# First AUGRU gates through the attention's two PSUM banks, and the keys of step 3 loaded in the phase change

## The chip, the cores and the metric

The kernel runs on one core of a Trainium2 chip. The metric is the device time of one execution in microseconds. Before the change it was 2062.48 us (median of 5 runs, 2060.84 to 2063.89).

## What is computed

A recommender block over 1024 users with a history of 100 steps of 128 features: a GRU over the history, an attention over the GRU's outputs ("keys"), a second GRU whose update gate is scaled by the attention (AUGRU), and a small MLP. Cut to what matters here:

```python
_, gru_seq = jax.lax.scan(gru_step, h0, swapaxes(history, 0, 1))
keys = swapaxes(gru_seq, 0, 1)
...
attn = softmax(where(mask == 1, score, -inf), axis=1)[..., 0]
pooled = einsum('bt,btd->bd', attn, keys)
att_seq = pooled.T[:T]                 # one weight per step and user
def augru_step(h, inp):
    x_t, a_t = inp
    ti = concatenate([h, x_t], axis=-1)
    r = sigmoid(ti @ aug_Wr.T + aug_br)
    u = sigmoid(ti @ aug_Wu.T + aug_bu)
    h_hat = tanh(concatenate([h * r, x_t], axis=-1) @ aug_Wh.T + aug_bh)
    u = a_t[:, None] * u
    h_new = (1.0 - u) * h + u * h_hat
```

The weight `a_t` of step t is feature t of the pooled vector, so no AUGRU state can be formed before the pooling over all 100 steps is complete. With h = 0 the first step needs only the gates of `x_0` and `a_0`: h = a_0 * sigmoid(u) * tanh(h_hat).

## The kernel before

Everything is fp32, features on the 128 partitions and users along the free dimension, in two halves of 512 users (`i` = 0, 1). There are two phases, each written out by hand: the order of the calls in the program is the order of the instructions in each engine's queue, and an instruction waits by semaphore for what it reads and for the last reader of the buffer or PSUM bank that it writes.

**The GRU phase** (`gru_phase`) runs 100 steps of the GRU, and beside them the attention's MLP, the softmax in blocks and the pooling. It holds six PSUM banks for gates (0 to 5) and two for the attention (6 and 7). After the last step the six banks are handed out again for the end of the attention: bank 2 and its neighbours hold products of the pooling (`kw`, L599 and L600), scores and exponents. The attention's two banks are read last by ACT at L704. DVE pools half 1, POOL half 0. At the end L937 (DVE) writes the pooled rows of half 1 and then half 0 into `s_b`, and eight stores, four for each half, bring them to `pooled_d` in DRAM: L941 issues half 1's four and one of half 0's on SP's queue; the other three of half 0 are issued on ACT's queue at L1204, in the next phase.

**The AUGRU phase** (`augru_phase`) sorts users by length, so that later steps run over fewer columns. Its widths come from a table, one of three (two lines, one line, full width), chosen by a branch at L1251 and L1252. The inputs take the two-line table. The phase starts so:

1. `load_key(0, i)`: four PE transposes (L1036) of gathered GRU outputs into one PSUM bank, and a copy by ACT (L1037) into a `k3` tile.
2. `first_step(i)`: for each half two matmuls (L977, `pu` and `ph`) and ACT's sigmoid and tanh on them (L979). Each of the four has a bank of its own, `EARLY_BANKS` = 2, 5, 6, 0.
3. `load_key(1, i)`, then the three stores on ACT's queue (L1204), then `gather_weights`: eight gathers on POOL (L144, `att_r`), four for each half, which read `pooled_d` in sorted order.
4. `open_gates(1, 1)` and `open_gates(1, 0)`: the key's part of step 1's three gates for each half, six matmuls (L1050), then `load_key(2, i)`.
5. `first_state(0)`: the row of weights of step 0 is spread over the partitions by four matmuls with the identity (L992) from half 0's `att_r`, and DVE makes the state of half 0 (L1003, L1004). `first_weights(0)` does the same for step 1's weights. Half 1 follows inside the first half step.
6. The loop over steps 1 to 99, with a `half_step` for each half: the state's part of the gates (L1054), ACT's sigmoids (L1074, L1075) and tanh (L1062), DVE's products (L1078 to L1091), the opening of the next gates, and the loads of step t + 2 (`load_att`, `load_key`). From step 8 on the keys come as rows that POOL gathers (L168, paced by a copy of the last `rest`, L167) and that DVE transposes (L1040).

The PSUM banks of this phase are seven pools of one bank (`ps3_0` to `ps3_6`) and `pa3` with one. By their places in PSUM `ps3_6` and `pa3` are the attention's two banks, and `ps3_0` to `ps3_5` the six others. `bank(name, n)` takes bank n; without n the next of a ring.

## Time and profile before

| | us |
|---|---|
| median of 5 runs | 2062.48 (2060.84 to 2063.89) |
| the profiled execution | 2061.72 |
| its span (first to last instruction) | 2059.8 |
| PE busy in it | 2026.3 |
| DVE / POOL / ACT busy | 1749.4 / 1303.3 / 831.0 |
| mean granted clock of PE | 0.995 |
| last transposes of the GRU phase's end to the first gates: PE without work | 1437.1 to 1447.1 |

The profile is of one execution. A row names an engine, a line, the tile written and those read, and a duration; the figure in brackets is the idle time of the engine before it and who ended it. "issue" means that the profile shows nobody for it. PE is TensorE, PEld its weight loads, ACT ScalarE, POOL GpSimd, and SPq or ACTq a DMA issued on that queue. The fp32 matmul stands in it as two rows (x2). PE's granted clock is 1 at full speed and 0.5 at half.

### The profile page before, as it was taken

The numbers are of one execution on the slowest core, as the hardware profiler recorded it, in microseconds if no ns is written. First come the engines' busy times: TensorE is split into PE (matmuls) and PEld (weight loads), VectorE is DVE, ScalarE is ACT, GpSimd is POOL, SyncE is SP. The second block draws the span as 40 slices with busy tenths as digits, with TensorE's granted clock in tenths as the row PEclk, the third lists the DMA queues.
The fourth block names the chain that finished last, engine by engine and source line by source line (L and its number), as shares of the span: only waits on it lengthen the run. The fifth ranks groups of instructions, "written<-read, shape, count | busy, mean of one in ns | idle before, by whom it ended". The sixth has DMA issues, their size and how long they took to land. (4 is left out here: it accounts for less than half of the span.)

```text
span 2059.8 us, 26800 instructions
## 1 busy us (share of the span) xinstructions
PE 2026.3 (98%) x8320; PEld 978.7 (48%) x8320; DVE 1749.4 (85%) x3050; ACT 831.0 (40%) x1516; POOL 1303.3 (63%) x1299
## 2 busy tenths in 40 slices
PE   8999999999999999999999999998899999999997
PEld 3343333333333333333333333334444556679997
DVE  6888999998989888988889888999467777888886
ACT  3333343333433343433333343343344444455554
POOL 0233939669796959596897868898545444444332
PEclk9999999999999999999999999999899999999999
DMA  4643333323334333333333333323334333333332
GB/s 119 117 94 89 103 103 97 93 81 97 111 106 103 116 107 114 111 106 102 103 98 95 104 96 96 104 90 114 107 102 113 96 92 96 94 97 101 88 77 36
DMA packets 254132, 204.36 MB, mean 99 GB/s; under 512 B 76006, under 2 KB 217034, under 8 KB 253978
## 3 DMA queue, kind: packets, MB, share of 16 engines
q1 hardware_dynamic: 240266, 170.43, 29.4%
q0 software_dynamic: 12128, 31.91, 5.5%
q8 instruction: 68, 1.11, 0.2%
q14 instruction: 86, 0.70, 0.1%
q10 hardware_dynamic: 1584, 0.20, 0.1%
HBM read 146.43 MB, written 54.40 MB: 97 GB/s over the span
## 5 line engine op out<-in xcount | busy, mean ns | idle before, releaser
L501 PE MATMUL ps<-x,wih 128*128 128x512 f32 x1200 | 592.8, 603 | 4.0 <-DMA x<-in_hist_x 4.0
L501 PE MATMUL ps<-hn,whh 128*128 128x512 f32 x1188 | 574.4, 592 | 0.0
L501 PEld LDWEIGHTS ps<-x,wih 128*128 128x128 f32 x1200 | 220.9, 191 | 327.7 <-issue 252.3
L501 PEld LDWEIGHTS ps<-hn,whh 128*128 128x128 f32 x1188 | 225.7, 190 | 284.2 <-issue 274.3
L487 POOL TENSOR_TENSOR xm<-x,m 128x512 f32<-128x512 f32 x200 | 248.7, 1244 | 137.2 <-DMA m<-mask_d 136.9
L532 ACT ACTIVATE ps<-ps,bih 128x512 f32<-128x512 f32 x200 | 132.4, 662 | 479.4 <-DVE ps L531 479.4
L513 ACT ACTIVATE r<-ps,brz 128x512 f32<-128x512 f32 x200 | 137.5, 688 | 380.0 <-PE ps L501 379.2
L488 POOL TENSOR_TENSOR hist<-hist,xm 128x512 f32<-128x512 f32 x200 | 267.8, 1339 | 15.7
L600 POOL TENSOR_TENSOR pooled<-pooled,kw 128x512 f32<-128x512 f32 x191 | 254.3, 1332 | 15.0
L599 POOL TENSOR_TENSOR kw<-kt,e 128x512 f32<-128x512 f32 x191 | 219.1, 1147 | 64.7 <-DVE e L772 64.6
L168 POOL DMA_INDIRECT rows<-keys_d,idx_k x204 | 198.7, 974 | 82.1 <-POOL rows L167 50.4
L576 DVE TENSOR_TENSOR kq<-hn,item 128x512 f32<-128x512 f32 x200 | 226.3, 1171 | 0.0
L663 PE MATMUL pm<-hn,wk 128*32 128x512 f32 x1200 | 211.8, 596 | 3.2 <-ACT q L242 1.6
L663 PE MATMUL pm<-kq,wkq 128*32 128x512 f32 x1200 | 209.4, 592 | 0.0
L1062 ACT ACTIVATE c<-ph,bh 128x96 f32<-128x96 f32 (+41 forms) x198 | 96.5, 487 | 254.5 <-PE ph L1054 229.4
L663 PE MATMUL pm<-mv,w 128*32 128x512 f32 (+1 forms) x808 | 196.3, 598 | 0.9 <-DVE e L753 0.9
L697 DVE TENSOR_TENSOR f<-pm,q 128x512 f32<-128x512 f32 x200 | 128.3, 683 | 52.7 <-PE pm L663 52.5
L167 POOL COPY rows<-rest 128x1 f32<-128x1 f32 x204 | 38.6, 189 | 202.1 <-DVE rest L1091 197.9
L1078 DVE TENSOR_TENSOR pu<-pu,c 128x96 f32<-128x96 f32 (+41 forms) x197 | 88.3, 448 | 91.3 <-ACT c L1062 82.2
L536 DVE TENSOR_TENSOR d<-hn,ps 128x512 f32<-128x512 f32 x198 | 135.9, 687 | 34.9 <-ACT ps L532 32.5
L537 DVE TENSOR_TENSOR d<-ps,d 128x512 f32<-128x512 f32 x200 | 138.3, 692 | 23.7 <-ACT ps L533 6.8
L531 DVE TENSOR_TENSOR ps<-ps,u 128x512 f32<-128x512 f32 x200 | 140.0, 700 | 21.6 <-PE ps L501 0.5
(180 smaller groups left out, 3017.7 us busy)
## 6 DMA issues: line engine op xcount, KB each, us to landing
x<-in_hist_x SPq DMA_DIRECT2D x212, 256.0 KB
keys_d<-kt SPq DMA_DIRECT2D x46, 1024.0 KB
m<-mask_d SPq DMA_DIRECT2D x200, 128.0 KB
keys_d<-kt SPq DMA_DIRECT2D x64, 64.0 KB
rows<-keys_d,idx_k POOLq DMA_INDIRECT x204
s_b<-mv SPq DMA_DIRECT2D x200, 8.0 KB
at<-att_d SPq DMA_DIRECT2D x34, 48.0 KB
mask_i<-in_mask SPq DMA_DIRECT2D x8, 200.0 KB
```

The costliest lines, as they stand in the source:

```text
L168: nc.gpsimd.indirect_dma_start(out=r[:, k, :], out_offset=None, in_=keys_d[q], in_offset=bass.IndirectOffsetOnAxis(ap=idx_k[:, k, i : i + ...
L487: nc.gpsimd.tensor_mul(d, x, m)
L488: nc.gpsimd.tensor_add(acc, acc, d)
L501: nc.tensor.matmul(p, lhsT=w[:, g, :], rhs=v, start=(j == 0), stop=(j == len(parts) - 1),)
L513: nc.scalar.activation(r, pr, AF.Sigmoid, bias=brz[:, 0:1])
L531: nc.vector.tensor_add(pi, pi, u)
L536: nc.vector.tensor_sub(d, h, pi)
L537: nc.vector.tensor_mul(d, pz, d)
L576: nc.vector.tensor_mul(kq, h, item[:, self.cols])
L599: eng.tensor_mul(d, k, w)
L600: eng.tensor_add(acc, acc, d)
L663: nc.tensor.matmul(p[i][s, :], lhsT=w[:, s], rhs=v, start=start, stop=stop)
```

## The change

```diff
-EARLY_BANKS, LATE_BANKS = (2, 5, 6, 0), (3, 4, 1)
+FREE_BANK, EARLY_BANKS, LATE_BANKS = 6, (2, 5, 6, 0), (3, 4, 1)
...
-        qp = pools.enter_context(tc.tile_pool(name="qp3", bufs=3 * NH))
+        qp = pools.enter_context(tc.tile_pool(name="qp3", bufs=4 * NH))
...
             for j, (n, f) in enumerate((("u", AF.Sigmoid), ("h", AF.Tanh))):
-                p = bank(f"p{n}", EARLY_BANKS[NH * i + j])
+                if j:
+                    p = pa.tile([P, HB], F32, tag="a", name=f"p{n}")
+                else:
+                    p = bank(f"p{n}", FREE_BANK)
...
-            if t + 2 < T:
+            if 1 < t < T - 2:
                 load_key(t + 2, i)
...
         for i in range(NH):
-            load_key(0, i, (None, EARLY_BANKS[NH])[i])
+            load_key(0, i, (None, FREE_BANK)[i])
         gates = [first_step(i) for i in range(NH)]
         for i in range(NH):
-            load_key(1, i, (EARLY_BANKS[0], None)[i])
+            load_key(1, i, (FREE_BANK, None)[i])
         for to, t in later["att", 0][: G - 1]:
             nc.scalar.dma_start(out=to, in_=t)
         sorted_rows = [gather_weights(i) for i in range(NH)]
+        for i in range(NH):
+            load_key(2, i, (FREE_BANK, None)[i])
         open_gates(1, 1, EARLY_BANKS)
         open_gates(1, 0, LATE_BANKS)
         for i in range(NH):
-            load_key(2, i)
+            load_key(3, i)
```

The first gates and the transposes of the keys of steps 0, 1 and 2 all go through banks 6 and 7. The keys of step 2 are transposed ahead of step 1's gates and not behind them. The keys of step 3 are loaded in the phase change, through bank 7, and no longer in the two half steps of step 1. There are two more `k3` tiles. In the changed kernel the lines of the AUGRU phase stand four to six lower: L977 is L981, L1036 L1040, L1037 L1041, L992 L996, L1054 L1058, L1204 L1208.

## Prediction

> **What bounds the kernel now.** I read the page first, then a table of six stretches around the phase change, then the timeline there. The page:

> ```profile
> span 2059.8 us, 26800 instructions
> PE 2026.3 (98%) x8320; PEld 978.7 (48%) x8320; DVE 1749.4 (85%) x3050; ACT 831.0 (40%) x1516; POOL 1303.3 (63%) x1299
> PEclk9999999999999999999999999999899999999999
> ```

> PE is the bound: 98% busy, and in the slices its one dip before the end, with the one lower clock digit, is where the GRU phase hands over to the AUGRU phase, about 1440 us. So only what shortens PE's stream, or the stretch in which PE has no work, can count. The stretches (us; length, then busy PE, PEld, DVE, ACT, POOL; granted clock, DMA share, GB/s):

> ```profile
> 1437.10:1447.10 10.00, 0.00 (x0) 0.00 (x0) 9.11 (x23) 2.84 (x5) 9.38 (x9) 0.65 0.56 169
> 1447.10:1457.30 10.20, 9.29 (x24) 4.50 (x25) 1.27 (x2) 3.71 (x6) 0.00 (x0) 0.84 0.30 51
> 1457.30:1463.70 6.40, 4.26 (x21) 2.38 (x19) 0.00 (x0) 1.16 (x2) 4.85 (x6) 1.00 0.15 41
> 1463.70:1471.40 7.70, 7.61 (x32) 5.09 (x32) 4.10 (x7) 2.54 (x5) 2.80 (x3) 0.78 0.21 53
> 1480.00:1500.00 20.00, 20.00 (x61) 9.79 (x60) 12.29 (x20) 8.74 (x15) 16.12 (x29) 1.00 0.60 187
> ```

> PE does nothing for 10 us. In the next 10 us it works, while DVE and POOL stand almost still, so its work there isn't obviously on the path. After 1480 it is full. Which chain crosses? The timeline (start, length, engine, line; idle before in brackets):

> ```profile
> 1446.36 0.69 DVE L600 TENSOR_TENSOR pooled<-pooled,last 128x512 f32<-128x512 f32 x1
> 1447.08 1.29 DVE L937 TENSOR_TENSOR s_b<-used,pooled 128x512 f32<-128x512 uint8 x2
> 1447.15 2.05 PE L977 MATMUL pu<-k,wu 128*128 128x512 f32 x2 [10.07 <-issue]
> 1447.80 2.49 SPq L941 DMA_DIRECT2D pooled_d<-s_b  x5
> 1452.46 0.69 ACT L979 ACTIVATE first_h<-ph,bh 128x512 f32<-128x512 f32 x1 [0.17 <-PE ph L977]
> 1453.39 0.35 ACTq L1204 DMA_DIRECT2D pooled_d<-s_b  x1
> 1453.79 1.05 ACTq L1204 DMA_DIRECT2D pooled_d<-s_b  x2
> 1457.33 0.99 POOL L144 DMA_INDIRECT att_r<-pooled_d,idx  x1 [10.46 <-issue]
> 1463.70 0.51 PE L992 MATMUL first<-ident,att_r 128*128 128x128 f32 x2 [0.75 <-DMA att_r<-pooled_d,idx]
> 1465.05 0.69 DVE L1004 TENSOR_TENSOR h<-first,first_h 128x512 f32<-128x512 f32 x1
> 1471.42 1.12 PE L1054 MATMUL pr<-h,wr 128*128 128x510 f32 x2
> ```

> The profile says "issue" for PE's 10.07 us. In the order of the program the first gate matmul waits for the count that the last DVE L600 sets; that ends at 1446.36 + 0.69 = 1447.05, and PE starts 0.10 later: bank 2, which the gate writes, was a pooling buffer until then. ACT therefore finishes the four first gates at 1453.15 and dispatches the key copies of step 1 by 1453.4. Behind these in ACT's queue stand three of the eight stores of the pooled rows, though their data was ready when the second L937 ended, at 1448.37. POOL's gathers need all eight stores. So the path is: DVE pooling, gates, ACT's queue, stores, gathers, first state, and from 1471.42 PE back to back.

> **The change, part by part.** *First gates in banks 6 and 7.* These were the attention's, whose last reader (ACT L704) ends at 1429.86; the wait for DVE leaves the first gate, which now waits for ACT's second key copy (end 1440.02). One 512-column gate is two passes: 0.43 us each at full clock, 0.85 at half clock (rows of 1450.54 and 1447.15). ACT has loaded its table by 1441.32. With two banks for four gates, PE waits for ACT's 0.69 us twice. At the clocks that I expect (half from 1440.6 to 1444.0, after 3.5 us without work as in the row of before), the gates' matmuls end about 1445.3, ACT's last gate 1446.2, the key copies of step 1 are dispatched by 1447.0. [...] I take the row: the stores issue at 1448.4 to 1449.85 (their 1.45 us of before), and **what is late next is DVE's pooling**.

> *The stores.* SP's five end issuing at 1450.29 as before; ACT's three now go out beside them. In a table of stretches of a quarter us, the DMA share falls to nothing at 1451.27 after SP's five and at 1455.8 after ACT's three: 0.98 and 0.96 us from issue end to last byte. If issue alone counted, the last byte would come at 1451.3: 4.5 us earlier. [...] That is 1455.8 - 1451.8 = **4.0 us** earlier. I take 4.0, with 3.0 and 4.6 as ends. POOL has waits for all eight in a row, and from last byte to its first gather it took 1.5 us; I leave that.

> *Gathers, first state.* Eight gathers at 1.26 us on POOL, landing about 1.5 us after each: nothing changes, all move by 4.0. First landing of half 0 complete: 1459.7 instead of 1463.70. No other DMA is moved past: SP's order is the same, and POOL's L168 row gathers start after the same `rest`.

> *PE until then.* After the gates: keys of steps 1, 2, then six gates of step 1 (5.1 us), then keys of step 3. The keys of step 2 are copied by ACT behind its stores, at 1449.9 to 1451.1; the third gate of half 1 shares bank 6 and waits for the first of these copies, about 0.7 us; behind it stand three gates and step 3's keys. Key 3 goes twice through one bank: (0.44 + 0.2 + 0.58) x 2 = 2.4 us. PE and ACT are done about 1456.6. The cover is the gathers' flight to 1459.7, 3.1 us of slack: cost nothing. If PE ran at half clock throughout, six gates take 10.2 us from 1448.2, and with the keys it ends about 1461.5: 1.8 us of the gain lost.

> *Keys of step 3 out of step 1.* Two times 0.44 us of PE (four transposes) and 0.58 of ACT leave. The first (1469.80) goes where PE then waits anyway for half 1's state (DVE, 1471.36): nothing. The second (1477.11) lies in the back-to-back stretch: **0.44 us**, full. The two more `k3` buffers bring no instruction, and no new late wait stands in the program: nothing.

> *Clock at the first half step.* By the granted clock in stretches of 1 us PE was at half clock from about 1464.0 to 1467.4, after sparse work. It will be sparse again for the same 4 us of gathers, so I expect the same. Ends: 0.3 us less, since half 1's gathers land only by 1468.6, or one window more, 3.4 x 0.5 = 1.7 us more. I take 0.

> Sum: 4.0 + 0.44 = 4.4, rounded with POOL's shorter row of waits after ACT's last store to 4.5 us. The profiled execution took 2061.72 (span 2059.8, 1.9 around it), so 2057.2 for it; the median of the runs is 0.8 higher, 2062.48, so **2058.0**. From 1480 on PE is full, so the shift is carried to the end.

> **The rivals.**
> A, as summed: 2058.0, chance 0.68. For it: the 0.10 us between DVE's end and PE's start, and the row of ACT's stores right behind ACT's gates. Its own spread (stores 3.0 to 4.6, clock) is 2056.5 to 2059.4.

> B, the gap isn't the bank's: PE stood for another reason (its code still to come, while DMA was full to 1442.7, for one), and the stores leave ACT as late as before. Then only the keys count: 2062.0, chance 0.09. Against it: ACT went through its branch, copied keys and loaded its table in that time.

> C, PE becomes the late one: at half clock through the six gates, it loses 1.8 of 4.5, or the first half step pays one more window, 1.7: about 2059.7, chance 0.18. For it: the work before the gathers is more broken up than before. Against it: six gates in a row from 1448 to 1454, enough by the row (3.3 us) to raise the clock.

> D, slower: the clock stays at half into the steps, because PE's work is thinner from 1440 to 1460. Each us of half clock in the full stretch costs 0.5; it takes 9 us to undo the gain, 17 us for 2066.7. The longest half-clock stretch with work in this trace is 3.5 us. Chance 0.05, about 2067.

> **How the numbers follow.** A measurement of this kernel can tell about 0.2%, 4.1 us, from no change; faster means below 2058.4. A lies just beyond that: I give about 0.49 of its 0.68 to faster, and C's lower edge 0.01: 0.50. Same: the rest of A and C, and B: 0.45. Slower: 0.05. The range of 8 in 10 takes A whole and C: 2056.2 to 2060.4; B and D are left out.

> **What would show it.** Right: PE's first gate at about 1440.2 with no wait for DVE; L1208's three stores at 1448.4 to 1449.9, beside SP's; DMA share near 1 from 1448.7 to 1451.8; POOL's first `att_r` gather at 1453.3 (1457.33); the last of half 0's `first` transposes at about 1459.7; no `pk` in step 1; every step from 2 on 4.4 us earlier. Wrong: a first gate still at 1447; `first` transposes waiting for ACT's key copies instead of the gathers (C); half clock beyond 4 us of work after the first state (C, D); stores that end after 1452.5.

## The result, and the profile after

The changed kernel takes 2058.15 us (median of 26 runs, 2056.66 to 2060.78), beside 2061.88 for the kernel before (46 runs). The ratio is 0.9982, with an interval of 0.9976 to 0.9987: 3.7 us faster, between 2.7 and 4.9. The gain is clear of the noise, but a little short of the 0.2% (4.1 us) from which on the prediction calls a kernel faster; by that bound it falls under "same", to which the prediction gave 0.45, and 0.50 to "faster". The predicted time was 2058.0.

The page of the changed kernel:

```profile
span 2056.5 us, 26797 instructions
PE 2027.3 (99%) x8320; PEld 978.7 (48%) x8320; DVE 1750.8 (85%) x3050; ACT 829.7 (40%) x1516; POOL 1300.6 (63%) x1299
PEclk9999999999999999999999999999999999999999
```

The span is 3.3 us shorter, and the one slice with a lower clock digit is gone (in the second execution of the changed kernel, below, it is there again). PE has the same 8320 matmuls and is busy 1.0 us longer (2027.3 against 2026.3), so the time has come out of PE's waiting: 29.2 us of the span instead of 33.5. The timeline of the changed kernel around the phase change shows where (start, length, engine, line, operation; in brackets the idle time before and its releaser):

```profile
1440.70 1.40 PE L981 MATMUL pu<-k,wu 128*128 128x512 f32 x2 [3.04 <-ACT k L1041]
1446.13 0.69 ACT L983 ACTIVATE first_h<-ph,bh 128x512 f32<-128x512 f32 x1 [0.17 <-PE ph L981]
1447.66 1.29 DVE L937 TENSOR_TENSOR s_b<-used,pooled 128x512 f32<-128x512 uint8 x2
1448.38 2.54 SPq L941 DMA_DIRECT2D pooled_d<-s_b  x5
1448.99 1.49 ACTq L1208 DMA_DIRECT2D pooled_d<-s_b  x3
1453.98 0.99 POOL L144 DMA_INDIRECT att_r<-pooled_d,idx  x1 [6.52 <-DMA pooled_d<-s_b]
1460.92 0.80 PE L996 MATMUL first<-ident,att_r 128*128 128x128 f32 x2 [0.98 <-DMA att_r<-pooled_d,idx]
1461.82 0.70 DVE L1007 TENSOR_TENSOR first<-first,first_u 128x512 f32<-128x512 f32 x1 [12.86 <-PE first L996]
1469.11 1.12 PE L1058 MATMUL pr<-h,wr 128*128 128x510 f32 x2 [0.66 <-DVE h L1008]
```

The first gate no longer waits for DVE; ACT's copy of a key releases it at 1440.70, 6.45 us earlier on the clock of the profile. ACT's last gate is done at 1446.82, before the pooled rows exist. So the three stores on ACT's queue go out at 1448.99, beside SP's five. POOL's first gather now waits for the stores alone.

In this execution DVE's pooling ended 0.58 us later than in the one before (L937 starts at 1447.66 against 1447.08). Across all the traces it starts between 1447.00 and 1449.08, in kernels whose DVE work up to there is the same. So I measure every trace from the start of L937 and cut the path behind it into four pieces, that end where the next begins: POOL's first gather; the first DVE operation of the first state (L1007); the state of half 1 (the second `h` of L1008); the first state part of `ph` (`ph<-r`, L1058; before, L1054) that is 486 columns wide, which lies in the full stretch, 74 to 81 us after L937.

| us | L937 to gather | to first state | to half 1's state | to the 486-wide step | sum |
|---|---|---|---|---|---|
| before | 10.25 | 6.99 | 6.35 | 55.34 | 78.93 |
| after | 6.32 | 7.84 | 6.54 | 54.90 | 75.60 |
| difference | -3.93 | +0.85 | +0.19 | -0.44 | -3.33 |

The first and the last piece are the change's two gains. The two in between give 1.04 us back. That the sum equals the difference of the spans is chance: L937 came 0.58 us later in this execution, and the rest behind the step took 0.55 us less (533.24 against 533.79). The windows of the changed kernel show one reason (length, busy PE, PEld, DVE, ACT, POOL; granted clock, DMA share, GB/s):

```profile
1453.00:1458.00 5.00, 3.62 (x17) 1.99 (x15) 0.00 (x0) 1.15 (x2) 3.10 (x4) 1.00 0.09 26
1458.00:1459.00 1.00, 0.25 (x2) 0.06 (x1) 0.00 (x0) 0.00 (x0) 0.74 (x1) 0.74 0.33 82
1459.00:1465.00 6.00, 4.88 (x14) 3.55 (x15) 1.39 (x2) 0.58 (x1) 3.80 (x4) 0.50 0.21 55
1465.00:1466.00 1.00, 1.00 (x3) 0.41 (x2) 0.00 (x0) 0.59 (x1) 0.00 (x0) 0.84 0.00 0
```

PE was at half clock for 6.8 us (0.52 of 1458 to 1459, six whole ones, 0.32 of the next), where the kernel before had 3.4. It fell before the last gathers had landed, so the last transposes of the first state (0.80 us a pair, where the kernel before took 0.51) ran at half clock too.

### The profile page after: what moved, and what is told of

Read it like the earlier page. It is cut to its first block, busy times and chain, and to the rows that moved or that the text cites. A ratio compares the mean times of both kernels' runs of the same rounds, so it can differ in the third digit from the quotient of the medians.

```text
span 2056.5 us, 26797 instructions
## 1 busy us (share of the span) xinstructions
PE 2027.3 (99%) x8320; PEld 978.7 (48%) x8320; DVE 1750.8 (85%) x3050; ACT 829.7 (40%) x1516; POOL 1300.6 (63%) x1299
## 3 DMA queue, kind: packets, MB, share of 16 engines
q8 instruction: 68, 1.11, 0.2%
## 5 line engine op out<-in xcount | busy, mean ns | idle before, releaser
L600 POOL TENSOR_TENSOR pooled<-pooled,kw 128x512 f32<-128x512 f32 x191 | 254.3, 1331 | 15.0
L168 POOL DMA_INDIRECT rows<-keys_d,idx_k x204 | 198.3, 972 | 82.3 <-POOL rows L167 49.7
```

The source lines that it names most:

```text
L168: nc.gpsimd.indirect_dma_start(out=r[:, k, :], out_offset=None, in_=keys_d[q], in_offset=bass.IndirectOffsetOnAxis(ap=idx_k[:, k, i : i + ...
L600: eng.tensor_add(acc, acc, d)
```

## The experiments

My theory: all of the gain is the earlier stores and the keys' 0.44 us, and what is missing is the half clock before and in the first half step. The rivals: the banks alone do it or the keys alone do it; the order of the stores alone would have done it; the missing part is something else than the clock. The experiments ran on other chips, where the kernel before takes 2058.1 to 2058.7 us; so ratios to it are compared, and pieces of the path.

**The banks alone.** The changed kernel with step 3's keys back in step 1 (the keys of step 2 keep their new place, ahead of step 1's gates; no run takes that apart from the banks):

```diff
-            if 1 < t < T - 2:
+            if t + 2 < T:
...
-        for i in range(NH):
-            load_key(3, i)
```

> The changed kernel with the keys of step 3 loaded in step 1 again; only the banks and the place of step 2's keys stay changed. Theory (stores freed from behind the gates, and 0.44 us of transposes out of the full stretch): the phase change keeps its 3.3 us, step 1 gives back 0.44, so about 2058.6 us, 0.4 above the changed kernel; first gates at 1440 to 1441, stores on ACT's queue at 1449. Rival (the keys carry the gain, the gap of PE has another cause): about 2061.5, as before.

2054.44 against 2058.12 us, ratio 0.9982 (0.9973 to 0.9991). A repeat on another chip gave the same:

> The changed kernel with the keys of step 3 in step 1, now beside the changed kernel on the same chip. Theory: 0.44 us slower than it, from the second trip's four transposes alone (0.44 us in the full stretch of step 1). Rival (the keys in the phase change lengthen the path or change the clock): equal or faster.

2054.90 against 2058.26, ratio 0.9983 (0.9974 to 0.9992). So the banks alone, with that place of step 2's keys, reach the whole ratio of the change, within the interval.

**The keys alone.** The kernel before with `load_key(3, i)` behind `load_key(2, i)`, the condition `1 < t < T - 2` and the larger pool:

```diff
-        qp = pools.enter_context(tc.tile_pool(name="qp3", bufs=3 * NH))
+        qp = pools.enter_context(tc.tile_pool(name="qp3", bufs=4 * NH))
...
         for i in range(NH):
             load_key(2, i)
+        for i in range(NH):
+            load_key(3, i)
```

> The kernel before with only the keys of step 3 moved into the phase change; gates, banks and stores as before. Theory: PE and ACT are already busy until half 0's gathers land (1463.7), so two trips through one bank (2.4 us) put the first transposes at about 1464.4 instead of 1462.0, 0.6 to 1.1 us on the path, and 0.44 comes back in step 1: 0.2 to 0.7 us slower than before, about 2062.3. Rival (these keys are a gain by themselves): 0.4 faster, 2061.4.

2059.99 against 2058.12, ratio 1.0007 (0.9998 to 1.0016): no gain, and by its median a loss. In its trace the sum is 80.88, 1.95 more than before. Of that, 0.77 lies ahead of the added keys: the early gates ran at half clock until 1451.87 in this execution, 4.87 us behind L937 (before: 3.30), and the gather came after 11.02. The timeline shows the rest:

```profile
1464.71 0.57 ACT L1037 COPY k<-pk 128x500 f32<-128x500 f32 x1 [0.75 <-PE pk L1036]
1465.38 1.92 PE L992 MATMUL first<-ident,att_r 128*128 128x128 f32 x8 [0.71 <-ACT k L1037]
```

The transposes of the first state wait for ACT's copy of step 3's key, and all four (eight rows) then run in one piece: the gathers had landed, and PE was late. With the first gates starting only behind the pooling, there is no room for more key work in front of the first state. The last piece is 54.91 us against 55.34, the 0.44 us of the prediction, but the piece up to the first state is 2.4 us longer (9.39).

**The stores alone.** The kernel before with the loop of ACT's three stores moved ahead of the first gates in ACT's queue:

```diff
+        for to, t in later["att", 0][: G - 1]:
+            nc.scalar.dma_start(out=to, in_=t)
         gates = [first_step(i) for i in range(NH)]
         for i in range(NH):
             load_key(1, i, (EARLY_BANKS[0], None)[i])
-        for to, t in later["att", 0][: G - 1]:
-            nc.scalar.dma_start(out=to, in_=t)
```

> The kernel before, with the three stores put ahead of the first gates in ACT's queue; banks and keys as before, PE's 10 us gap stays. Theory (two queues stand behind the gates: the stores and PE's own work): stores at 1448.4 to 1449.9, gathers about 4 us earlier, but PE is done with the gates and keys of steps 1 and 2 only at about 1462, so the first state comes 1.0 to 1.5 us earlier: about 2060.7. Rival (the stores alone are the path): 3.5 to 4 us, 2058.2. Rival (not ACT's queue at all): no change, 2061.9.

2057.04 against 2058.12, ratio 0.9995 (0.9986 to 1.0004): not told from no change. Its timeline:

```profile
1454.27 0.99 POOL L144 DMA_INDIRECT att_r<-pooled_d,idx  x1 [6.50 <-ACT first_u L979]
1454.43 0.69 ACT L979 ACTIVATE first_h<-ph,bh 128x512 f32<-128x512 f32 x1 [0.19 <-PE ph L977]
1464.01 1.13 PE L992 MATMUL first<-ident,att_r 128*128 128x128 f32 x8 [0.72 <-ACT k L1037]
```

The gather comes 6.28 us after L937, just as early as in the changed kernel. But the first state comes after 17.26, as late as before (17.24), since PE now reaches its transposes last: it still has gates, keys and six more gates to do from 1448.06 on. A part of that lateness is the clock's: in this execution the first gates ran at half clock until 1453.42, 5.43 us behind L937 (before: 3.30), and ACT's last gate and the transposes each come 1.06 us later behind L937 than before. Without that, by estimate, 1.0 us would be left of the 4 (17.24 less 16.20), which is the expected 1.0 to 1.5. So the 4 us are only to be had if PE's work before the first state moves as well. This is what the first gates' banks bring beyond the stores.

**The clock.** The changed kernel, with four fp32 matmuls of 512 columns in PE's queue ahead of the first state's transposes. Their product goes into `spare`, where it is overwritten, so they only keep PE busy:

```diff
         spare = bank("spare", EARLY_BANKS[-1])
+        for _ in range(4):
+            nc.tensor.matmul(spare, lhsT=ident, rhs=item[:, :HB], start=True, stop=True)
         first_state(0, pa.tile([P, HB], F32, tag="a", name="first"))
```

> The changed kernel with four more 512-column matmuls (3.4 us) on PE ahead of the first state's transposes, in the bank that these overwrite next, so that PE is not idle while the gathers fly; the output is the same. Theory (half clock from 1458.3 to 1465.2 costs part of the forecast gain): PE at full clock at the first state, the first sigmoid 1.2 us earlier, half 1's state 0.6 us earlier (then its gathers hold it): 0.6 to 1.2 us faster than the changed kernel, about 2057.3. Rival (the gathers alone set the end): no change, 2058.15; PE must be free by 1460.9 or it turns slower.

2053.10 against 2058.12, ratio 0.9976 (0.9966 to 0.9987). On a second chip, beside the changed kernel itself:

> The changed kernel with four more matmuls ahead of the first state's transposes, beside the changed kernel on the same chip; the output is the same. Theory (half clock costs 1.2 to 1.7 us of the forecast gain): 1.2 to 1.7 us faster than the changed kernel. Rival (the first look was favoured by early gathers): 0.5 or less.

> The changed kernel unaltered, on one chip beside the next three. Theory: 3.3 to 4.0 us faster than the kernel before; the half clock at the first half step lasts two windows (about 7 us) again, since the work before the first state is sparse in every execution; the landing of half 0's fourth gather, which in the first profile took 2.2 us after its issue and in two others 1.5, is chance.

The warm kernel 2053.39, ratio 0.9979 (0.9970 to 0.9988); the changed kernel 2055.19, ratio 0.9985 (0.9976 to 0.9994); before 2058.26. The two intervals overlap, but the 11 runs of each on this chip can be set side by side: the warm one is faster in 101 of the 121 pairs, by 1.5 us in the mean. Its mean granted clock over the runs is 0.9973, the changed kernel's 0.9961. The traces show where the time is: both warm executions have a sum of 73.88, against 75.60 and 76.61 in the two executions of the changed kernel. The changed kernel came out 3.1 us faster than before here, a little under its expectation of 3.3 to 4.0. Its two windows of half clock came again; and so did the late landing of half 0's fourth gather, which the expectation had called chance: the first state is 8.02 us behind the first gather. The timeline of the first warm one:

```profile
1456.51 3.60 PE L1218 MATMUL spare<-item,ident 128*128 128x512 f32 x8
1459.95 1.05 PE L996 MATMUL first<-ident,att_r 128*128 128x128 f32 x8
1462.59 1.12 PE L1058 MATMUL pr<-h,wr 128*128 128x510 f32 x2 [0.69 <-DVE h L1008]
```

and its windows:

```profile
1458.00:1459.00 1.00, 1.00 (x3) 0.38 (x2) 0.00 (x0) 0.00 (x0) 0.85 (x1) 1.00 0.26 66
1459.00:1465.00 6.00, 5.30 (x29) 3.54 (x28) 1.95 (x3) 1.64 (x3) 3.81 (x4) 1.00 0.20 55
```

The clock stays at 1.00, the pair of `pr` matmuls takes 1.12 us where the changed kernel's first took 2.07, and half 1's state comes 18.98 us after L937 instead of 20.70. The 3.60 us of added matmuls cost nothing: in the changed kernel PE is busy for 1.82 of the 3.42 us from 1455.06 on, and its last two pairs of transposes wait 0.89 and 0.98 us for their gathers.

**Short instead of long.** Is it the added instructions, by what they shift, or the work? The same four matmuls, of 8 columns (`spare[:, :8]`, `item[:, :8]`). This run was also to shift the loading of 16 KB of instructions that the trace shows in this stretch (in the changed kernel one packet between 1458.6 and 1458.8; 68 such packets in the whole run hold 1.11 MB):

> The changed kernel with four matmuls of 8 columns (not 512) where the warm one has its four long ones: as many instructions, hardly any work; the output is the same. It tells the two differences of the warm kernel apart. Theory 1 (half clock is the whole loss): half clock for 5 to 7 us at the first half step as in the changed kernel, the step that is compared within 0.3 us of the changed kernel's (75.6 and 76.6 us behind the second last DVE stage). Theory 2 (a 16 KB load of code, which falls 11.0 to 11.5 us behind that mark into the landing of half 0's fourth gather, delays it): the load moves to about 10.2, and the first state's first product on DVE comes 13.4 to 13.7 us behind the mark instead of 14.2 to 14.3, although the clock is as low.

2054.92 against 2058.66, ratio 0.9983 (0.9974 to 0.9992), and a sum of 75.53: the changed kernel's, not the warm one's. The clock in its windows is the changed kernel's as well:

```profile
1458.00:1459.00 1.00, 0.51 (x3) 0.30 (x2) 0.00 (x0) 0.00 (x0) 0.95 (x1) 0.84 0.33 78
1459.00:1465.00 6.00, 4.25 (x14) 3.47 (x15) 1.39 (x2) 0.58 (x1) 3.81 (x4) 0.50 0.22 55
```

So the warm kernel's gain is the PE work that fills the wait, not the place of its instructions. The expectation for the first state was too early: it came after 14.12 us and not after 13.4 to 13.7, because the last two transposes (four rows) started together, 6.53 us behind the first gather, at half clock.

**What half clock cost the kernel before.** Two of the 512-column matmuls in the kernel before, at the same place:

> The kernel before with two more 512-column matmuls on PE between the keys of step 2 and the first state's transposes (1461.1 to 1462.8 us of its profile, when PE waits anyway); the output is the same. Theory (the half clock of 3.5 us cost the kernel before little, since half 1's gathers land late): 0.2 to 0.5 us faster than before, so that of the warm kernel's 5.0 us nearly all is the change's. Rival (before pays for half clock as much as the changed kernel): 1.2 us faster.

2057.78 against 2058.66, ratio 0.9997 (0.9988 to 1.0006): not told from no change. In its trace the sum is 78.91, as before, from two things that cancel. The early gates ran longer at half clock in this execution (from 1449.15 to 1453.86; before from 1447.15 to 1450.38), so the stores left ACT later and the gather came after 10.98 us. That lies ahead of the added matmuls. Behind the gather it is 67.93 us to the step and not 68.68: 0.75 less, with the clock at 1.00 throughout. That lies between the theory's 0.2 to 0.5 and the rival's 1.2, and each side is one trace.

**The order of the stores.** The changed kernel with the three stores on SP's queue, behind SP's five:

```diff
-            nc.scalar.dma_start(out=to, in_=t)
+            nc.sync.dma_start(out=to, in_=t)
```

> The changed kernel with the three stores on SP's queue behind its five. Theory (what the change wins is the stores' issue, and two queues save issue time): SP issues eight at 0.5 us, to 1.5 us after its five; the last byte comes 0.6 to 1.0 us later than with two queues, and the whole is 0.6 to 1.0 us slower than the changed kernel, still about 3 us faster than before. Rival (the engines' share is the limit, not the issue): no difference.

2054.86 against 2058.26, ratio 0.9985 (0.9976 to 0.9994), where the changed kernel beside it had the same ratio. The gather comes 7.31 us after L937 instead of 6.31 and 6.32, so the second queue is worth 1.0 us to the stores. The sum is 76.46, within what two executions of the changed kernel differ by (75.60, 76.61): the runs can't show this 1.0 us at the end.

## Why the prediction was right, and where it was off

The pieces of all the traces that the points rest on:

| us | L937 to gather | to first state | to half 1's state | to the step | sum |
|---|---|---|---|---|---|
| changed kernel, second chip | 6.31 | 8.02 | 7.38 | 54.90 | 76.61 |
| banks alone | 6.30 | 7.18 | 6.98 | 55.34 | 75.80 |
| banks alone, again | 6.36 | 7.32 | 6.15 | 55.33 | 75.16 |
| keys alone | 11.02 | 9.39 | 5.56 | 54.91 | 80.88 |
| stores alone | 6.28 | 10.98 | 5.56 | 55.33 | 78.15 |
| warm | 6.33 | 7.03 | 5.62 | 54.90 | 73.88 |
| warm, again | 6.25 | 7.12 | 5.61 | 54.90 | 73.88 |
| short matmuls | 6.26 | 7.86 | 6.51 | 54.90 | 75.53 |
| stores on SP | 7.31 | 7.36 | 6.88 | 54.91 | 76.46 |
| before, warm | 10.98 | 6.99 | 5.61 | 55.33 | 78.91 |

- *The first gates.* The bank was the cause: with other banks the gate starts at 1440.70 (predicted 1440.2), and rival B, the gap of another cause, falls. The half clock of the early gates lasted 3.42 us in this execution (1441.41 to 1444.83; I had 1440.6 to 1444.0), and not through all four gates. The 3.5 us without work from which I had 1440.6 is in neither trace: half clock began 3.06 us behind PE's last transpose in the kernel before (1440.14) and 3.75 us behind it in the changed one. That it ended so early was luck: in the second traces of the changed kernel and of the banks alone it lasted 6.83 us, into the fourth gate (with the stores on SP there was none). There too the gather came 6.31 and 6.36 us after L937, so even the longer half clock cost nothing, though barely: in the changed kernel's second trace ACT takes its second key copy at 1449.25, and the pooled rows are ready at 1449.40. The stores issued at 1448.99 to 1450.48, which is the predicted 1448.4 to 1449.85 moved by the 0.58 of DVE's later end. What is late next is DVE's pooling, as predicted.
- *The stores.* Last byte 4.59 us after L937 instead of 8.72: 4.1 us against the predicted 4.0. The gather came 3.93 earlier, since POOL took 1.73 from there and not 1.53. No run shows the term under the 4.0, a share of 1 as the limit, from which I had the last byte at 1451.8; measured is 1452.25, or 1451.67 less the 0.58 of DVE's later end. The eight stores took 3.27 us of all 16 engines (3.06 in the kernel before, five and three apart) in 3.01 us from first to last byte, with a share of up to 1.39, so the nearness of 4.0 is in part luck. And 10.25 for the kernel before is a favourable execution; the two other traces with its first gates and stores have 10.98 and 11.02.
- *PE until then.* The slack held. The last copy of step 3's key ends at 1457.22 (1456.6 predicted), and the last pair of transposes waits 0.98 us for its gather at 1460.92. The experiments on the keys alone and the stores alone show that the cover was needed: there the transposes wait for the key copies.
- *Keys out of step 1.* 0.44 us predicted, and 0.42 to 0.44 measured in every pair: 55.33 or 55.34 us with the keys in step 1, 54.90 or 54.91 without. In the runs it can't be seen (0.9985 with, 0.9983 without, side by side).
- *"Gathers, first state: nothing changes, all move by 4.0."* This failed by 0.57 us. From its first gather to the last pair of half 0's transposes the kernel before needs 6.37 us, the changed one 6.94.
- *"Clock at the first half step ... I take 0."* This term was mis-sized, by 0.47 us in the profiled pair: 0.28 at the last pair of transposes (0.90 us from their start to DVE's, at full clock 0.62) and 0.19 up to half 1's state. The half clock stretch doubled from 3.41 to 6.83 us, the one window more of rival C, but only a part of it lies on the path. The full price of half clock behind the gather is 0.75 us in the kernel before, by one pair of traces. In the changed kernel it is, together with the late landing, 1.73 us (69.28 from gather to step, against 67.55 warm), and 2.75 in its execution on the second chip. The price isn't stable: the stretch lasted 3.41 to 10.24 us across the five other traces of the new first gates without long added matmuls.

The sum in the profile: 3.93 + 0.44 - 0.57 - 0.47 = 3.33 us, where 4.5 was forecast. In the medians it is 3.7 of 4.5, so 0.8 us went missing; in the traces it is these two terms, which I had taken as 0. That the median came within 0.2 us of the forecast owes something to the reference: I worked from 2062.48, and the kernel before, run more often, has 2061.88.

What stays open is the late landing. In four traces the last pair of half 0's transposes waits for its own gather and starts 6.27 to 6.42 us from the first gather (before, before warm, and both of the banks alone); in the two executions of the changed kernel it starts after 6.94 and 7.12. In these two the trace shows the 16 KB load of instructions 4.6 and 5.0 us from the first gather, while the fourth gather is in flight; in the kernel before it comes 7.3 us from the first gather, behind the landing, and with two matmuls added to that kernel at 5.8, with no late landing. That is a coincidence in time in a few traces. In the run that was to move the load it came at 4.2, and the last two transposes could start after 6.53, but nothing of it was gained at the first state, for the half clock took it back. So the cause isn't shown.

The version with the four 512-column matmuls is the best one, ratio 0.9976 and 0.9979 to the kernel before on two chips.

## What to carry to other kernels

A wait that the profile calls "issue" can be the hand-over of a PSUM bank, as here 10.07 us of PE, of which 3.04 were left with other banks: find in the program which buffer the instruction writes, and whose last reader ends just before it starts. When a transfer on the path is brought forward, look at once at what the other engines still have to do before they can use it: here the stores alone and the keys alone each gave nothing that could be told, while with the earlier gates the first gather, and with it the first state, came some 4 us earlier in the banks-alone kernel. Where PE waits a few us for a transfer with only scattered short work, matmuls into a free bank that are sized to end when the transfer lands are worth a try: here four of 512 columns (3.60 us) kept the clock at 1.00 for the work behind them, where it was 0.50, and cost nothing in two traces (first state 7.03 and 7.12 us from the first gather, against 7.84 and 8.02).

## What the runs showed of the hardware that I had not expected

```profile
1460.62:1464.03 3.41, 1.89 (x13) 1.49 (x14) 0.00 (x0) 0.58 (x1) 2.50 (x4) 1.00 0.15 38
1464.03:1467.45 3.42, 3.42 (x12) 2.43 (x11) 1.39 (x2) 0.59 (x1) 2.47 (x3) 0.50 0.26 62
```

```profile
1455.06:1458.48 3.42, 1.82 (x10) 1.01 (x8) 0.00 (x0) 1.15 (x2) 2.60 (x3) 1.00 0.21 58
1458.48:1461.89 3.41, 1.77 (x6) 1.47 (x7) 0.07 (x1) 0.00 (x0) 2.50 (x4) 0.50 0.17 43
1461.89:1465.30 3.41, 3.41 (x11) 2.21 (x10) 1.32 (x2) 0.58 (x1) 1.56 (x2) 0.50 0.22 58
1465.30:1468.72 3.42, 3.15 (x17) 1.79 (x15) 2.38 (x4) 1.56 (x3) 0.00 (x0) 1.00 0.08 19
```

```profile
1455.73:1459.15 3.42, 3.13 (x11) 1.70 (x12) 0.00 (x0) 0.81 (x2) 2.51 (x3) 1.00 0.23 62
1459.15:1462.56 3.41, 2.75 (x19) 2.08 (x17) 1.39 (x2) 0.51 (x1) 2.80 (x3) 1.00 0.20 58
```

Each square's clock went with the work in the one before it. Of the squares of the twelve traces around the phase change, all 19 at half clock with PE busy for 95% or more were followed by full clock, and all 16 with 78% or less by half clock again. At full clock, all 16 squares with 43% or less were followed by half clock; of six squares with 48 to 57%, two were; above that only one was, with 75%, and it is the square with the four 8-column matmuls, of whose busy time 0.96 us is theirs. Without these it would be 47%. So in these traces the busy share of a whole square goes with the clock of the next, and one kernel had two squares at half clock behind the gathers in one execution and one in another (banks alone: from 1459.02 and from 1461.44), with the grid in another place. That the place of the grid decides it isn't shown. The warm kernel fills the square in which the changed one waits: 3.13 of 3.42 us busy, against 1.82.

**The stores of two queues passed a share of 1.** In the changed kernel's windows of a quarter us the share is about 1 while both queues issue, and rises to 1.39 for the us behind the last issue (SP's, 1450.92):

```profile
1450.00:1450.25 0.25, 0.25 (x2) 0.00 (x0) 0.00 (x0) 0.00 (x0) 0.00 (x0) 1.00 1.05 183
1451.00:1451.25 0.25, 0.10 (x1) 0.10 (x1) 0.00 (x0) 0.25 (x2) 0.00 (x0) 1.00 1.39 213
1451.75:1452.00 0.25, 0.25 (x2) 0.13 (x1) 0.00 (x0) 0.00 (x0) 0.00 (x0) 1.00 1.38 209
1452.25:1452.50 0.25, 0.25 (x2) 0.06 (x1) 0.00 (x0) 0.00 (x0) 0.00 (x0) 1.00 0.03 4
```

The last columns are the share of the 16 engines, which adds up the times that packets took, and GB/s. With all eight on SP's queue, the share goes up and down between 0.31 and 1.10, with eight peaks for the eight issues; of that kernel's windows:

```profile
1452.50:1452.75 0.25, 0.25 (x2) 0.06 (x1) 0.00 (x0) 0.00 (x0) 0.00 (x0) 1.00 0.31 51
1452.75:1453.00 0.25, 0.25 (x2) 0.08 (x1) 0.00 (x0) 0.00 (x0) 0.00 (x0) 1.00 1.10 192
```

The highest quarter with one queue is 192 GB/s at a share of 1.10, with two 214 at 1.39 (216 in the changed kernel's second trace). With one queue the last issue ends 4.81 us after L937, with two 3.26: 1.55 us, of which 1.0 is left at the first gather. How that 1.0 divides between issue time and rate isn't shown. The rate of the last us is 11% above the best of one queue. Whether that comes of the second queue or of more stores in flight at once isn't shown. A share of 1 was not the limit that I had reckoned with.
